# Selective scan: units of 32 channels by 16 states instead of 96 channels by 4, two groups of states in one scan instruction

## The chip, the cores and the metric

One core of a Trainium2 chip runs the whole program in one launch. The metric is device time in microseconds, the median of three runs. All numbers are 32-bit floats.

## The reference, cut to what matters

The model takes a batch of 8 images of 64x64 positions and 96 channels through four residual layers. Layers 0 and 2 are vision state-space layers with a selective scan, layer 1 is a chunked variant of it, layer 3 works on frequencies. The change lies in layers 0 and 2, so the scan runs 2 x 8 = 16 times in a launch. What it computes, for each image and each of K = 4 directions (rows, columns, and both backwards), over D = 192 channels, N = 16 states and L = 4096 positions:

```python
delta = softplus(delta + delta_bias)           # delta, B, C: projections of u
def step(h, inp):
    ut, dt, bt, ct = inp
    dA = jnp.exp(dt[..., None] * A4)           # decay, channel x state
    dBu = (dt * ut)[..., None] * bt[:, :, None, :]
    h = h * dA + dBu
    y = jnp.einsum('bkdn,bkn->bkd', h, ct)
    return (h, y)
...
return y + u * D[None, :, None]                # the four directions are added up
```

`u` is the output of a depthwise 3x3 convolution with SiLU.

## The kernel before, in words

An image's layer goes through `project` (norm and first projection), `selective_scan` and, at the start of the next layer, `back` (gate, norm, output projection, residual). `selective_scan` begins with the convolution: VectorE does rows 0 to 40 (`conv`, line 248), TensorE rows 40 to 64 in three blocks of 8 rows (`conv_pe`, line 264) with diagonal weights that GpSimd builds (`diagonals`, line 258). Each block's sums lie in the two banks named `pu`, of which there is one buffer, until ScalarE has applied SiLU.

Then come 32 steps: 4 directions by 8 chunks of 512 positions (`steps`). A step is 8 units: two halves of 96 channels, and in each four groups `g` of 4 states. On the 128 partitions lie 32 channels by 4 states; the third index `q` is a 32-channel third of the half. A unit does:

- `decays` (line 508): ScalarE writes three tiles `da` = exp(delta x A) into three PSUM banks, from `dx`, delta repeated over the states.
- `with_b` (line 520) and `with_b2` (line 528): `db` = delta x u x B. VectorE makes thirds 0 and 1, reading delta x u from the banks `pu`, where TensorE has spread it over the partitions (`spread`, line 498); GpSimd makes third 2 from `du2`.
- three scans of 512 columns on VectorE (line 633), which begin from the last column of the chunk before (`state`).
- `hc` = h x C for all three thirds on GpSimd (line 645).
- `total_y` (line 534): three matmuls with `red` add up the 4 states of a group into bank `py`. Four units fill it; then `add_y` (line 549) adds it to `y` on VectorE.

The inputs of a step are made by the generator `prepare` (line 429), one part at a time, beside the units of the step before (`PARTS`, line 25: parts at units -2, -1, 0, 1, 3 and 4, counted from that step's start). TensorE projects B and C (`pb`) and delta (`pv`) in two banks of their own, tag `misc`. ScalarE copies B and C to `bcs` and makes `delta` by softplus. Since B, C and delta must be repeated over partitions, they go to DRAM (`bcd`, `dd`, `dud`) and come back with a repeating source: `bc` (2 MB, two buffers), `dx` (0.79 MB a half, three buffers), `du2` (0.52 MB, two buffers). All of these are issued on the SyncE (SP) queue in program order.

The order on every engine is the order written in the code (`manual_schedule`); waits are put in where one tile's use needs them. Pools decide when a buffer comes free.

Of the kernel before, what the change touches and what calls it, by code (L numbers as in the profile page):

```python
# [24 lines left out]
PARTS = (-2, -1, 0, 1, 3, 4)  # L25
# [39 lines left out]
def tile_vision_stack(  # L65
# [51 lines left out]

    eps = wp.tile([128, 1], F32, name="eps")
# [29 lines left out]
    b2 = wp.tile([128, DM], F32, name="b2")  # L148
    with (
# [3 lines left out]

        wdts = []
        for i, (dtw, dtx) in enumerate(((dt0, dx0), (dt2, dx2))):
            left = sp.tile([RK, K * 192], F32, name="left")
            nc.sync.dma_start(left, dtx)
            right = sp.tile([RK, K * 192], F32, name="right")
            nc.sync.dma_start(right, dtw)
            wdt = wp.tile([DM, K, 2, 192], F32, name=f"wdt{i}")  # L160
            for k in range(K):
                pw = pp.tile([DM, 2, 192], F32, name="pw", bufs=2)
                for hf in range(2):
                    nc.tensor.matmul(
                        pw[:, hf, :],
                        left[:, k * 192 + hf * 96 : k * 192 + hf * 96 + 96],
                        right[:, k * 192 : k * 192 + 192],
                        start=True,
                        stop=True,
                    )  # L170
                nc.vector.tensor_copy(wdt[:, k, :, :], pw)
            wdts.append(wdt)
# [221 lines left out]
    def selective_scan(w, wdt, a, d, u, y):  # L394
# [11 lines left out]
        xproj = w[:, C_XP : C_XP + K * 2 * XR].rearrange("p (k j r) -> p k j r", k=K, j=2)  # L406
# [6 lines left out]
        units = 2 * NSG  # L413
        total = len(steps) * units
        with (
# [6 lines left out]
            tc.tile_pool(name="p_du", bufs=1, space=PSUM) as pup,  # L422
            tc.tile_pool(name="p_da", bufs=3, space=PSUM) as pap,
# [5 lines left out]
            def prepare(i):  # L429
# [4 lines left out]
                m = made[i] = {}  # L434
                pb = pmp.tile([128, 2, LC], F32, name="pb", tag="misc")
                for hf in range(2):
                    nc.tensor.matmul(
                        pb[:32, 0, :],
                        xproj[:, k, hf, RK:XR],
                        uv[hf],  # L440
                        start=(hf == 0),
                        stop=(hf == 1),
                    )
                yield
                bcs = tp.tile([32, LC], F32, name="bcs")
                nc.scalar.copy(bcs, pb[:32, 0, :])  # L446
                bcd = dp.tile([32, LC], F32, name="bcd")
                nc.sync.dma_start(bcd, bcs)
                pv = pmp.tile([128, 2, LC], F32, name="pv", tag="misc")
                for hf in range(2):  # L450
                    for hi in range(2):
                        nc.tensor.matmul(  # L452
                            pv[:DM, hf, :],
                            wdt[:, k, hi, hf * 96 : hf * 96 + 96],
                            uv[hi],
                            start=(hi == 0),
                            stop=(hi == 1),
                        )
                    yield

                m["bc"] = bc = cp.tile([128, 2 * NSG, LC], F32, name="bc")
                src = bcd.rearrange("(j n) l -> n j l", n=4)
                for n in range(4):
                    nc.sync.dma_start(
                        bc[32 * n : 32 * n + 32],
                        src[n : n + 1].to_broadcast([32, 2 * NSG, LC]),
                    )
                delta = tp.tile([DM, 2, LC], F32, name="delta")
                for hf in range(2):
                    bias = w[:, C_DTB + 2 * k + hf : C_DTB + 2 * k + hf + 1]  # L470
                    nc.scalar.activation(delta[:, hf, :], pv[:DM, hf, :], AF.Softplus, bias=bias)
                dd = dp.tile([192, LC], F32, name="dd")
                m["dx"] = []

                def repeat(hf):
                    nc.sync.dma_start(dd[hf * 96 : hf * 96 + 96], delta[:, hf, :])
                    dx = cp.tile([128, 3, LC], F32, name="dx", bufs=3)
# [4 lines left out]

                repeat(0)
                yield
                m["du"] = du = tp.tile([DM, 2, LC], F32, name="du")
                for hf in range(2):
                    nc.gpsimd.tensor_mul(  # L487
                        cut(du[:, hf, :], wh), cut(delta[:, hf, :], wh), uv[hf]
                    )
                dud = dp.tile([32, 2, LC], F32, name="dud")  # L490
                nc.sync.dma_start(dud, du[64:96])
                m["du2"] = du2 = cp.tile([128, 2, LC], F32, name="du2")
# [4 lines left out]

            def spread(t):

                m, hf = made[t // units], t % units // NSG  # L500
                m["pu"] = pu = pup.tile([128, 2, LC], F32, name="pu")
                for q in range(2):
                    rows = slice(32 * q, 32 * q + 32)
                    nc.tensor.matmul(  # L504
                        pu[:, q, :], sel[rows, :], m["du"][rows, hf, :], start=True, stop=True
                    )

            def decays(t):
                m, (k, _) = made[t // units], steps[t // units]
                hf, g = t % units // NSG, t % NSG  # L510
                m["da", t] = []
                for q in range(3):
                    da = pap.tile([128, LC], F32, name="da")
                    at = 3 * hf + q
                    nc.scalar.activation(  # L515
                        da, m["dx"][hf][:, q, :], AF.Exp, scale=av4[:, k, at, g : g + 1]
                    )
                    m["da", t].append(da)

            def with_b(t):  # L520
                m, g = made[t // units], t % NSG
                db = gp.tile([128, 2, LC], F32, name="db", bufs=2)
                nc.vector.tensor_mul(  # L523
                    db, m["pu"], m["bc"][:, g : g + 1, :].to_broadcast([128, 2, LC])
                )
                m["db", t] = db

            def with_b2(t):
                m, hf, g = made[t // units], t % units // NSG, t % NSG
                db = gp.tile([128, LC], F32, name="db2")  # L530
                nc.gpsimd.tensor_mul(db, m["du2"][:, hf, :], m["bc"][:, g, :])  # L531
                m["db2", t] = db

            def total_y(t):

                m, hf, g = made[t // units], t % units // NSG, t % NSG
                hc = m.pop(("hc", t))
                if g == 0:
                    sums.append((pyp.tile([DM, LC], F32, name="py"), hf, steps[t // units]))
                for q in range(3):  # L540
                    nc.tensor.matmul(  # L541
                        sums[-1][0][32 * q : 32 * q + 32, :],
                        red,
                        hc[:, q, :],
                        start=(g == 0),
                        stop=(g == NSG - 1),
                    )

            def add_y():
                py, hf, (k, c) = sums.pop(0)  # L550
                yv = view(y[:, hf, :], k % 2 == 1, c * LC, LC)
                if k == 0:
                    nc.vector.scalar_tensor_tensor(
                        yv, u[:, hf, c * LC : c * LC + LC], d[:, hf : hf + 1], py, ALU.mult, ALU.add
                    )
                else:
                    nc.vector.tensor_add(yv, yv, cut(py, k % 2 == 1))

            parts = {}
            for i in range(len(steps)):
                for n, at in enumerate(PARTS):
                    parts.setdefault(units * (i - 1) + at, []).append(i)
            going = {}

            def prepare_parts(t):
                for i in parts.get(t, ()):
# [5 lines left out]
            dg = cp.tile([128, 2 * NSG, LC], F32, name="bc").rearrange("p a b -> p (a b)")  # L574
            dg = dg[:DM, : 18 * DM].rearrange("p (n m) -> p n m", n=18)
            diagonals(dg, w)
            first = list(range(-units + PARTS[0], 0))

            def conv_block(n):
                acc = pup.tile([128, 2, LC], F32, name="pu")[:DM]  # L580
                for hf in range(2):
                    conv_pe(dg, y, n, hf, acc[:, hf, :])
                return n, acc

            def silu_block(n, acc):
                for hf in range(2):
                    silu(w, u, (8 * n, 8 * n + 8), hf, acc[:, hf, :])

            for hf in range(2):
                conv(w, y, u, (0, 8), hf)  # L590
            for _ in range(5):
                prepare_parts(first.pop(0))
            done = conv_block(5)
            for n, rows in ((6, (8, 24)), (7, (24, 40))):
                for hf in range(2):
                    conv(w, y, u, rows, hf)
                    if n == 6 and hf == 0:
                        prepare_parts(first.pop(0))
                        prepare_parts(first.pop(0))
                silu_block(*done)  # L600
# [715 lines left out]
```

## Time and profile before

| | |
|---|---|
| median of three runs | 32904.44 us (32891.0 to 32913.84) |
| the profiled execution | 32953.56 us, its span 32951.8 us |
| busy share of the span | VectorE 81%, TensorE 72%, GpSimd 70%, ScalarE 46% |
| granted TensorE clock, mean | 0.696 of full |
| products h x C on GpSimd (L645) | 14165.5 us, 4096 of 3458 ns |
| scans (L633) | 12980.4 us (10752 of 1261 ns) and 1762.9 us (1536 of 1203 ns) |
| DMA | 2672.97 MB, mean 81 GB/s |

A line of a group names the line of the code, the engine, the operation, output and inputs with their shapes and a count; then the busy time in us, the mean of one in ns, and how long the engine stood idle just before these instructions, with what ended most of it. PE is TensorE, PEld its weight loads, DVE VectorE, ACT ScalarE, POOL GpSimd, SP the queue that issues transfers. A timeline line begins with the start in us and the time in us. By the timeline of GpSimd a step takes 39.4 us where u is read in rows and 39.9 us where it is read in columns; 512 steps are over 60% of the span.

### The profile page before, as it was taken

What the parts mean: (1) busy time and instruction counts of PE and PEld (TensorE: products, weight loads), DVE (VectorE), ACT (ScalarE), POOL (GpSimd) and SP (SyncE); (2) the same over time, 40 slices, a digit from 0 to 9 for tenths busy, and PEclk for the clock granted to TensorE, in tenths of its full rate; (3) what the DMA queues carried; (4) which work ended last, traced back from release to release, by engine and by line L of the source; (5) the groups of instructions that cost most, each with busy time, mean ns of one, the idle gap of its engine ahead of it and who ended that gap; (6) DMA issues with size and microseconds to landing.
All of it is one profiled execution on the core that took longest, in us unless ns stands there. A gap on an engine that the chain in (4) does not pass through costs nothing. (4 is left out here: it accounts for less than half of the span.)

```text
span 32951.8 us, 294593 instructions
## 1 busy us (share of the span) xinstructions
PE 23737.3 (72%) x90246; PEld 8381.8 (25%) x90246; DVE 26605.5 (81%) x27030; ACT 15241.2 (46%) x24909; POOL 23212.3 (70%) x12908
## 2 busy tenths in 40 slices
PE   6686766967668676686766967668676686766867
PEld 1141311413114131141311413114131141311413
DVE  9859698596986969859698596985969859698696
ACT  5435454354543545435454354543545435454354
POOL 8739587395874949739487395873948739497494
PEclk6676766767667676676766767767676676766767
DMA  5315253152431525315253152531525315253152
GB/s 114 85 26 122 59 113 86 25 121 60 112 87 29 121 62 113 82 29 121 57 114 83 25 121 60 113 85 27 121 59 114 84 28 121 59 115 83 30 122 57
DMA packets 1461625, 2672.97 MB, mean 81 GB/s; under 512 B 271544, under 2 KB 271768, under 8 KB 1460048
## 3 DMA queue, kind: packets, MB, share of 16 engines
q1 hardware_dynamic: 1443408, 2647.83, 36.0%
q8 instruction: 724, 11.86, 0.2%
q10 hardware_dynamic: 16640, 6.29, 0.1%
q14 instruction: 853, 6.99, 0.1%
HBM read 2271.62 MB, written 381.68 MB: 81 GB/s over the span
## 5 line engine op out<-in xcount | busy, mean ns | idle before, releaser
L645 POOL TENSOR_TENSOR hc<-h,bc 128x1536 f32<-128x1536 f32 x4096 | 14165.5, 3458 | 678.1 <-DVE h L633 676.5
L633 DVE TENSOR_TENSOR_SCAN h<-da,state,db 128x512 f32<-128x512 f32 x10752 | 12980.4, 1261 | 102.5 <-POOL hc L645 100.7
L541 PE MATMUL py<-hc,cst 128*32 128x512 f32 x24576 | 6836.1, 905 | 7754.8 <-POOL hc L645 7100.7
L515 ACT ACTIVATE da<-dx,a2s 128x512 f32<-128x512 f32 x6144 | 4208.3, 690 | 4489.7 <-DVE h L633 4486.1
L515 ACT ACTIVATE da<-dx,a0s 128x512 f32<-128x512 f32 x6144 | 4208.3, 690 | 4489.2 <-DVE h L633 4485.1
L523 DVE TENSOR_TENSOR db<-pu,bc 128x1024 f32<-128x1024 f32 x4096 | 4931.0, 1204 | 597.6 <-ACT da L515 415.1
L531 POOL TENSOR_TENSOR db<-du,bc 128x512 f32<-128x512 f32 x4096 | 5330.2, 1301 | 103.5 <-DMA du<-dud 103.5
L541 PEld LDWEIGHTS py<-hc,cst 128*32 128x32 f32 x24576 | 805.3, 129 | 13702.4 <-POOL hc L645 13459.6
L452 PE MATMUL pv<-u,wdt 96*96 96x512 f32 x4096 | 2932.4, 845 | 22.0 <-ACT bcs L446 22.0
L226 POOL TENSOR_SCALAR xn<-xs,sb 96x512 f32<-96x512 f32 x192 | 215.2, 1127 | 3215.7 <-DVE sb L206 3078.3
L818 POOL TENSOR_TENSOR rr<-lr,cst 128x768 f32<-128x768 f32 x256 | 433.3, 1693 | 2354.1 <-ACT lr L816 1231.2
L887 ACT ACTIVATE sg<-sg 128x768 f32<-128x768 f32 x1024 | 819.3, 800 | 2467.3 <-PE sg L871 2467.3
L504 PE MATMUL pu<-du,cst 32*128 32x512 f32 x4096 | 1848.0, 994 | 4.0 <-DVE db L523 4.0
L633 DVE TENSOR_TENSOR_SCAN h<-da,db 128x512 f32<-128x512 f32 x1536 | 1762.9, 1203 | 62.5 <-POOL hc L645 60.7
L487 POOL TENSOR_TENSOR du<-delta,u 96x512 f32<-96x512 f32 x1024 | 1445.0, 1443 | 0.0
L919 DVE TENSOR_TENSOR wt<-wt,cbm 128x768 f32<-128x768 f32 x1024 | 1092.8, 1087 | 352.0 <-ACT wt L888 348.5
L957 PE MATMUL py<-wt,xdt 128*32 128x128 f32 x12288 | 1024.4, 334 | 230.0 <-DVE y L995 154.2
L1078 DVE SCALAR_TENSOR_TENSOR f<-p,w3bs,f 128x512 f32<-128x512 f32 x768 | 576.4, 750 | 726.1 <-ACT f L1071 699.1
L965 PE MATMUL py<-ce,state 96*96 96x128 f32 x3968 | 1124.6, 373 | 0.0
L452 PEld LDWEIGHTS pv<-u,wdt 96*96 96x96 f32 x4096 | 615.9, 170 | 1903.2 <-issue 1410.0
L292 POOL TENSOR_SCALAR xn<-xs,sb 96x512 f32<-96x512 f32 x192 | 156.6, 818 | 1318.4 <-issue 953.3
L871 PE MATMUL sg<-rr,lr 32*128 32x384 f32 x4096 | 1073.3, 644 | 0.0
(201 smaller groups left out, 31992.8 us busy)
## 6 DMA issues: line engine op xcount, KB each, us to landing
bc<-bcd SPq DMA_DIRECT2D x2048, 512.0 KB, 10.1
dx<-dd SPq DMA_DIRECT2D x4096, 192.0 KB, 3.6
du<-dud SPq DMA_DIRECT2D x2048, 128.0 KB, 2.7
dd<-delta SPq DMA_DIRECT2D x1024, 192.0 KB, 4.3
dud<-du SPq DMA_DIRECT2D x512, 128.0 KB, 1.9
xd<-xs SPq DMA_DIRECT2D x256, 192.0 KB, 2.1
bcd<-bcs SPq DMA_DIRECT2D x768, 64.0 KB, 1.6
xs<-xd SPq DMA_DIRECT2D x128, 384.0 KB, 5.8
```

Source lines behind the costliest of these rows:

```text
L452: nc.tensor.matmul(pv[:DM, hf, :], wdt[:, k, hi, hf * 96 : hf * 96 + 96], uv[hi], start=(hi == 0), stop=(hi == 1),)
L487: nc.gpsimd.tensor_mul(cut(du[:, hf, :], wh), cut(delta[:, hf, :], wh), uv[hf])
L504: nc.tensor.matmul(pu[:, q, :], sel[rows, :], m["du"][rows, hf, :], start=True, stop=True)
L515: nc.scalar.activation(da, m["dx"][hf][:, q, :], AF.Exp, scale=av4[:, k, at, g : g + 1])
L523: nc.vector.tensor_mul(db, m["pu"], m["bc"][:, g : g + 1, :].to_broadcast([128, 2, LC]))
L531: nc.gpsimd.tensor_mul(db, m["du2"][:, hf, :], m["bc"][:, g, :])
L541: nc.tensor.matmul(sums[-1][0][32 * q : 32 * q + 32, :], red, hc[:, q, :], start=(g == 0), stop=(g == NSG - 1),)
L633: nc.vector.tensor_tensor_scan(h[:, q, way], das[q][:, way], db2[:, way] if q == 2 else db[:, q, way], init, ALU.mult, ALU.add,)
L645: nc.gpsimd.tensor_mul(hc, h, m["bc"][:, NSG + g : NSG + g + 1, :].to_broadcast([128, 3, LC]))
L871: nc.tensor.matmul(live[e]["sg"][:, p, :3, :], m["lr"][rows, 0, :], m["rr"][rows, 3 * p : 3 * p + 3, :], start=True, stop=True,)
L919: nc.vector.tensor_mul(it["wt"], it["wt"], m["cbm"][:, j : j + 1, :].to_broadcast([128, RK, Q]),)
L965: nc.tensor.matmul(py[:, i, hf, :], it["before"][:, 96 * hf : 96 * hf + 96], m["ce"][:, j, :], start=False, stop=True,)
```

## The change

A unit is now 32 channels by all 16 states, so that a step has 6 units (`units = NCG`) instead of 8. The four groups of 4 states lie side by side in the free dimension, 513 apart (`SEG`): 512 positions, and one place in between.

- `db` and `h` are tiles of 4 x 513 + 1 columns. The place ahead of each group holds the state from the chunk before, written into `db` by ScalarE (`enter`), and `da` holds 0 there; so one scan instruction runs over two groups, 1026 columns, from an initial 0.0, and restarts in the middle. A unit is two scans instead of three.
- `da` is two PSUM tiles of 1027 columns, one for each pair of groups.
- `with_b` is one instruction of 4 x 512 columns a unit: on VectorE for four units of a step, on GpSimd for the two with `n % 3 == 2`.
- The product with C (`leave`) is one instruction of 4 x 512 on GpSimd and is done in place, `h` by `h`; ScalarE's copy of the last column goes before it. `h` has five buffers.
- `total_y` runs once per half, after its third unit: 12 matmuls with `red`, behind one that starts the sum with `y` itself (identity) or, in direction 0, with u x D (`skip`). ScalarE copies the bank to `y`; the two sums on VectorE (`add_y`) are gone.
- The projections use the one bank of the sums (tag `py`), delta's second half by itself, and its first half together with B and C as 128 columns of weights (`wdts`, which lie in DRAM and are loaded at the start of each layer). They are copied to `raw1` and `raw0`; softplus works in place.
- `bc` is split: `c` has two buffers, `b` one. `dx` has two instead of three, `du2` one instead of two. The parts of `prepare` are eight: raw1's matmuls in unit 4 of the step before the previous one, its copy in unit 5; then, in the previous step, raw0's matmuls in unit 1, its copy with `bcd` and `c` in unit 2, softplus with `dd` and the first `dx` in unit 2, `b` in unit 3, du with `dud` and `du2` in unit 4, the second `dx` in unit 5.
- In the prologue the blocks of the convolution on TensorE have two buffers of their own (`p_conv`), and block 6 is issued before the SiLU of block 5.

The core of the diff:

```diff
-        units = 2 * NSG
+        units = NCG
...
+                yield
+                raw0 = tp.tile([128, LC], F32, name="raw0")
+                nc.scalar.copy(raw0, pv)
                 bcd = dp.tile([32, LC], F32, name="bcd")
-                nc.sync.dma_start(bcd, bcs)
+                nc.sync.dma_start(bcd, raw0[DM:])
+                def copies(at, pool, name):
+                    t = pool.tile([128, NSG, LC], F32, name=name)
+                    src = bcd[at : at + NST].rearrange("(g n) l -> n g l", n=4)
+                    for n in range(4):
+                        nc.sync.dma_start(
+                            t[32 * n : 32 * n + 32],
+                            src[n : n + 1].to_broadcast([32, NSG, LC]),
+                        )
+                    return t
-                m["bc"] = bc = cp.tile([128, 2 * NSG, LC], F32, name="bc")
...
+                m["c"] = copies(NST, cp, "c")
+                yield
+                delta = [raw0[:DM], raw1[:DM]]
...
+                    nc.scalar.activation(delta[hf], delta[hf], AF.Softplus, bias=bias)
...
+                nc.sync.dma_start(dd[:DM], delta[0])
                 repeat(0)
+                nc.sync.dma_start(dd[DM:], delta[1])
                 yield
+                m["b"] = copies(0, tp, "b")
+                yield
...
+            def enter(t):
+                i, n = t // units, t % units
+                k, c = steps[i]
+                first = c == (0 if k < 2 else NCH - 1)
+                db = gp.tile([128, NSG * SEG + 1], F32, name="db")
+                src = zero if first else states[i - 1][:, NSG * n : NSG * n + NSG]
+                nc.scalar.copy(places(db, NSG, int(k >= 2)), src)
+                made[i]["db", n] = db
...
+            def with_b(t):
+                m, n = made[t // units], t % units
+                pool = n % 3 == 2
+                (nc.gpsimd if pool else nc.vector).tensor_mul(
+                    groups(m["db", n]),
+                    (m["du2"][:, n // 3, :] if pool else m["pu"])
+                    .unsqueeze(1).to_broadcast([128, NSG, LC]),
+                    m["b"],
+                )
...
+            def scan(t, p):
...
+                at = slice(2 * p * SEG + rev, 2 * (p + 1) * SEG + rev)
+                if p == 0:
+                    made[i]["h", n] = gp.tile([128, NSG * SEG + 1], F32, name="h", bufs=5)
+                nc.vector.tensor_tensor_scan(
+                    made[i]["h", n][:, at][:, way],
+                    das[p][:, rev : 2 * SEG + rev][:, way],
+                    made[i]["db", n][:, at][:, way],
+                    0.0, ALU.mult, ALU.add,
+                )
+            def leave(t, more):
...
+                nc.scalar.copy(
+                    states[i][:, NSG * n : NSG * n + NSG], h[:, :, 0 if k >= 2 else LC - 1]
+                )
+                if more:
+                    prepare_part(i + 1)
+                nc.gpsimd.tensor_mul(h, h, made[i]["c"])
...
+                for t in range(total + 2):
+                    n, i = t % units, t // units
+                    ahead = t + 1 < total
+                    if n == 1 and t + 2 < total:
+                        spread(t + 2)
+                    elif n in (0, 3, 5) and ahead:
+                        spread(t + 1)
+                    if n == 0 and i > 0:
+                        sums = total_y(i - 1, 1)
+                    elif n == 3:
+                        sums = total_y(i, 0)
+                    elif n == 1:
+                        prepare_part(i + 1)
+                    elif n == 4:
+                        prepare_part(i + 2)
+                    if t < total:
+                        scan(t, 0)
+                        if n % 3 == 0 and t + 2 < total:
+                            with_b(t + 2)
+                    if ahead:
+                        decays(t + 1, 0)
+                    if n % 3 == 1 and t > 1:
+                        nc.scalar.copy(*sums)
+                    if t < total:
+                        scan(t, 1)
+                        leave(t, n == 4)
+                    if t + 3 < total:
+                        enter(t + 3)
+                    if ahead:
+                        decays(t + 1, 1)
+                        if (n + 1) % 3 != 2:
+                            with_b(t + 1)
+                    if n == 2:
+                        prepare_part(i + 1)
+                        prepare_part(i + 1)
+                    elif n == 3:
+                        prepare_part(i + 1)
+                    elif n == 5:
+                        prepare_part(i + 1)
+                        prepare_part(i + 2)
```

## The prediction, made before the changed kernel was run

> **What bounds the kernel now.** I read the page first, then the busy time by windows inside one scan, the timelines of GpSimd and of the DMA queue over one step, and the DMA rate in slices of 2 us. The page's costliest groups:
>
> ```profile
> L645 POOL TENSOR_TENSOR hc<-h,bc 128x1536 f32<-128x1536 f32 x4096 | 14165.5, 3458 | 678.1 <-DVE h L633 676.5
> L633 DVE TENSOR_TENSOR_SCAN h<-da,state,db 128x512 f32<-128x512 f32 x10752 | 12980.4, 1261 | 102.5 <-POOL hc L645 100.7
> L523 DVE TENSOR_TENSOR db<-pu,bc 128x1024 f32<-128x1024 f32 x4096 | 4931.0, 1204 | 597.6 <-ACT da L515 415.1
> L531 POOL TENSOR_TENSOR db<-du,bc 128x512 f32<-128x512 f32 x4096 | 5330.2, 1301 | 103.5 <-DMA du<-dud 103.5
> L633 DVE TENSOR_TENSOR_SCAN h<-da,db 128x512 f32<-128x512 f32 x1536 | 1762.9, 1203 | 62.5 <-POOL hc L645 60.7
> ```
>
> 4096 units are 512 steps of 8. Busy time by windows in the first scan (PE, PEld, DVE, ACT, POOL, clock, DMA share, GB/s):
>
> ```profile
> 160.00:1390.00 1230.00, 775.93 (x2096) 133.15 (x2096) 1208.21 (x1053) 669.37 (x1142) 1230.00 (x558) 0.64 0.53 119
> ```
>
> GpSimd never rests, VectorE rests 1.8%, DMA is half idle. A step is 18 GpSimd instructions, so 558 are 31 steps: **39.67 us a step**. The GpSimd timeline gives pitches (start to start):
>
> ```profile
> 713.62 3.06 POOL L487 TENSOR_TENSOR du<-delta,u 96x512 f32<-96x512 f32 x2
> 716.59 3.50 POOL L645 TENSOR_TENSOR hc<-h,bc 128x1536 f32<-128x1536 f32 x1
> 720.00 1.32 POOL L531 TENSOR_TENSOR db<-du,bc 128x512 f32<-128x512 f32 x1
> 721.22 3.49 POOL L645 TENSOR_TENSOR hc<-h,bc 128x1536 f32<-128x1536 f32 x1
> ```
>
> 1536 columns take 3.4 us, 512 take 1.23: 2.11 ns a column and 0.15 fixed. The two du take 2.97 here, 2.45 where u is read in rows.
>
> Now the DMA queue in one step, and the DMA share and GB/s (last two columns) of slices inside it:
>
> ```profile
> 730.78 0.31 SPq L448 DMA_DIRECT2D bcd<-bcs  x1
> 733.97 2.88 SPq L464 DMA_DIRECT2D bc<-bcd  x4
> 741.06 0.31 SPq L476 DMA_DIRECT2D dd<-delta  x1
> 749.54 1.72 SPq L480 DMA_DIRECT2D dx<-dd  x4
> ```
> ```profile
> 734.00:736.00 2.00, 2.00 (x9) 0.63 (x10) 2.00 (x3) 0.50 (x3) 2.00 (x2) 1.00 0.29 88
> 736.00:738.00 2.00, 0.95 (x3) 0.09 (x1) 2.00 (x2) 1.27 (x2) 2.00 (x1) 1.00 0.87 126
> 738.00:740.00 2.00, 0.50 (x6) 0.18 (x6) 2.00 (x3) 1.75 (x3) 2.00 (x3) 1.00 1.07 167
> 740.00:742.00 2.00, 2.00 (x10) 0.30 (x4) 2.00 (x3) 1.97 (x4) 2.00 (x1) 0.72 0.90 190
> 742.00:744.00 2.00, 1.07 (x5) 0.19 (x6) 2.00 (x3) 1.99 (x3) 2.00 (x2) 0.50 1.05 209
> 744.00:746.00 2.00, 1.17 (x6) 0.00 (x0) 2.00 (x3) 0.96 (x3) 2.00 (x2) 0.50 1.07 202
> 746.00:748.00 2.00, 0.14 (x3) 0.14 (x6) 2.00 (x3) 1.16 (x2) 2.00 (x2) 0.50 0.59 131
> 748.00:750.00 2.00, 1.78 (x6) 0.06 (x3) 2.00 (x3) 1.03 (x3) 2.00 (x2) 0.50 0.11 34
> ```
>
> This is the view that decides. The eight slices move 2.29 MB, which is bc (2.10) and the small dd (0.19), at about 200 GB/s once full. The dd store is issued at 741.06, yet dx, which reads dd back, goes out only at 749.54: a small store queues behind the big load, and the issue queue stands until it has landed. Here nobody waits: bc has two buffers, dx three.
>
> **The compute engines, part by part.** *GpSimd.* The columns stay: 6 products with c and 2 with b of 2048 instead of 8 of 1536 and 8 of 512. At 2.11 ns and 0.15 each is 4.47 us: 35.8 + 2.7 (du) = 38.5 us, 1.2 less, eight fixed costs. No row has groups at a step of 513; the row nearest in kind that reads its operand in steps is du at 1.48 against 1.22, so 38.5 to 46; I take 38.5, since only one hop in 512 columns is new.
>
> *VectorE.* 12 scans of 1026 columns that start from 0.0: twice the pitch of 512 is 2.24, less the fixed part; I take 2.2 (2.1 to 2.4). Four products of 2048: 2.2 each (row L523: 1.12 for 1024). Sum 35.2 against 8 x (1.12+3.54) + two sums into y (0.64 to 1.16 each) = 39.6. So VectorE alone would run 4.4 us faster.
>
> *ScalarE* gets the two copies into y (0.58 by the copies of a 96x512 bank) and initial values (0.18 each); 24 exponentials at 0.62 leave it some 60% busy. *TensorE.* The sums of a half come as 12 matmuls after its third product, four triples of 1.71 us at half clock, 7 us, plus an identity matmul ahead, which doesn't need h. Its cover: between product 5 and product 1 GpSimd has two instructions (8.9 us) and the way over TensorE (7.0), the copy (0.6) and the state copy (0.2) takes some 8.3; hidden, by 0.6. If the cover is gone it is a stall of that size.
>
> **The DMA chain, where I put the time.** The projections of the next step now share the bank of the sums, so bcs becomes raw0, copied only in unit 2, behind both exponentials of unit 3, which wait for unit 2's second scan. Call its end X. And b has one buffer, loaded behind c, dx and two dd stores in the in-order issue queue:
> - raw0 ready: state 0.18, initial value 0.18, two exponentials 1.3, copy 0.57, handoffs: X+2.4.
> - bcd stored, c issued 1.9 later (60.82 to 62.73 in the first prologue): X+4.3.
> - bc to dx took 15.6 (733.97 to 749.54); c is 1.05 MB less, 5.2 us at 200 GB/s (by the slices 1.25 MB are through after 8.5, and landed after 9.5): 10.0, so dx leaves at X+14.3.
> - dx (0.79 MB) took 4.5 until its slices end at 754: X+18.8. The second dd, 0.19 MB: X+19.8. b, 1.05 MB at 200 GB/s: X+25.0, landed X+25.7.
> - VectorE's product of unit 0 waits for b, and behind it stand all scans. From it to the end of unit 2: two products and six scans, 8 x 2.2 = 17.6. That end is the next X.
>
> A step is thus **43.3 us**. Whatever is late for 38.5 on GpSimd hides in this. Bounds: at 167 GB/s (slice 738) c and b take 1.1 longer each, 45.5; at 253, the best slice seen with dx (764 to 766), 1.1 shorter each, 41.1. The end on the other side is b hidden: it must be there by X+20.9 for GpSimd's 38.5, by X+22.6 to match today. The next loads, dud and du, follow b by some 6 us, but GpSimd needs them only for unit 2, 11 us after b: hidden.
>
> *A rule against this reading.* The Trainium skill, "DMA: Bandwidth & Descriptors", section "Bandwidth", puts the 16 engines' ceiling near 436 GB/s. By it the chain's 3.28 MB would need 7.5 us instead of 16.4, b would be there before X+17, and the change would win as in the first rival. The slices above, full at 200, speak against it.
>
> **The prologue** gains. VectorE ends its share of the convolution at 107.0 and stands still until 133.44 (26.41 us, 16 times 415.1 in the row of L523), because the third convolution block on TensorE waits for the bank of the second until 109.41 and takes 18.3. With two banks it follows the second (85.22 + 15.5, plus 1.7 for a projection) and ends near 118; SiLU, table and two exponentials later the first scan starts at about 121.3, not 135.7. Between nothing and 20 us gained; I take 14.
>
> **Sum.** First X: 121.3 + one product and six scans = 136.7. Then 31 x 43.3, and behind the last X five GpSimd instructions, 22.8: 1501.8, where today the last product ends at 1406.7. That is 95.1 more in each of 16 layers, 1520 us. The profiled execution takes 32953.6 (span 32951.8), 49 above the median of 32904.4: 34474 there, **34425** as a median. By the chain's bounds and the prologue's, 33300 to 35600.
>
> **Rivals.** *The chain is hidden and GpSimd bounds* (transfers run faster when halved, or overlap). Start of products at 125.9 + 4 of stalls + 32 x 38.5 - 4.5 = 1357, 50 less a layer: about 32100, faster. For it: 128 to 192 KB loads land in 2.7 to 3.6 us. Against: the slices. It decides below X+22.6. *dd doesn't queue behind c*: then volume alone counts, 5.6 + 16.4 + 0.7: b at X+22.7, a step of 40.3, 32940. For it: dd lands in 4.3 at the median. Against: 8.5 behind bc. *c and b crawl* at 126 GB/s, the slice of 736: 3.1 longer each, 49.5, 37500; against it, that slice is the ramp.
>
> **How the numbers follow.** The chain 0.70; hidden 0.12; dd beside c 0.13, a third of it on each side of no change; crawling 0.05. About 0.2% is what a measurement can tell. Faster 0.16, same 0.04, slower 0.80. Half of the hidden case and the crawl stay outside 32700 to 35700.
>
> **What would show it.** Right: VectorE idle some 8 us a step before its product with b of unit 0, released by the DMA of b; GpSimd no longer at 100% and waiting for scans or du; 2048 columns at 4.5 us, scans at 2.2; SP waiting for dd about 7 us a step. Wrong: GpSimd at 100%, or VectorE waiting for GpSimd or TensorE instead, or products with c well above 4.5 us.

## The result: no gain and no loss worth naming, and the profile after

The changed kernel takes 32878.98 us (median of 12), the kernel before 32916.47 in the same runs: a ratio of 0.9984, interval 0.9972 to 0.9996. That is 0.16% faster, less than the 0.2% that the prediction took as the least a measurement can tell. The forecast was 34425, slower by 4.6%, so the likeliest case was wrong by 1550 us. The time lies below the 33300 to 35600 that came from the bounds of the chain and the prologue, and only inside the wider 32700 to 35700 of the chances. The profiled execution below took 32765.36 (span 32763.6).

The costliest groups, which answer to those shown of before (line engine op, shapes, count | busy, mean ns | idle before, what ended it):

```profile
L572 DVE TENSOR_TENSOR_SCAN h<-da,db 128x1026 f32<-128x1026 f32 x6144 | 13651.3, 2278 | 210.0
L593 POOL TENSOR_TENSOR h<-h,c 128x2048 f32<-128x2048 f32 x3072 | 12784.8, 4169 | 620.3 <-ACT state L588 490.6
...
L542 DVE TENSOR_TENSOR db<-pu,b 128x2048 f32<-128x2048 f32 x2048 | 4654.1, 2272 | 2062.5 <-DMA b<-bcd 2057.1
...
L542 POOL TENSOR_TENSOR db<-du,b 128x2048 f32<-128x2048 f32 x1024 | 4648.7, 4540 | 1705.4 <-PE pu L536 644.8
```

Busy time of the engines in the window of the first scan that was shown of before (PE, PEld, DVE, ACT, POOL, clock, DMA share, GB/s):

```profile
160.00:1390.00 1230.00, 817.02 (x2094) 185.03 (x2094) 1093.85 (x494) 726.48 (x1343) 1123.39 (x307) 0.69 0.48 118
```

GpSimd worked all of the 1230.00 us before; now it works 1123.39, and VectorE went from 1208.21 to 1093.85. Both have less to do and both stand still for over 100 us. What VectorE stands still for is in its group: 2057.1 us in front of the product with b, ended by the DMA of b. That is the wait which the prediction named. The timeline of VectorE in one step (start, duration, instruction, idle before it) shows it come once a step:

```profile
737.43 2.27 DVE L542 TENSOR_TENSOR db<-pu,b 128x2048 f32<-128x2048 f32 x1
739.80 4.48 DVE L572 TENSOR_TENSOR_SCAN h<-da,db 128x1026 f32<-128x1026 f32 x2
744.20 2.27 DVE L542 TENSOR_TENSOR db<-pu,b 128x2048 f32<-128x2048 f32 x1
746.57 8.85 DVE L572 TENSOR_TENSOR_SCAN h<-da,db 128x1026 f32<-128x1026 f32 x4
760.02 2.29 DVE L542 TENSOR_TENSOR db<-pu,b 128x2048 f32<-128x2048 f32 x1 [4.60 <-DMA b<-bcd]
```

The queue of SyncE in the same step:

```profile
739.69 0.31 SPq L465 DMA_DIRECT2D bcd<-raw  x1
741.35 1.73 SPq L472 DMA_DIRECT2D c<-bcd  x4
743.18 0.38 SPq L493 DMA_DIRECT2D dd<-raw  x1
748.58 1.72 SPq L490 DMA_DIRECT2D dx<-dd  x4
750.39 0.37 SPq L495 DMA_DIRECT2D dd<-raw  x1
750.87 1.91 SPq L472 DMA_DIRECT2D b<-bcd  x4
```

The small store dd is issued right behind c, and dx, which reads it back, leaves 5.4 us later. So the chain raw0, bcd, c, dd, dx, dd, b is there, in the forecast's order. But from c to dx it takes 7.23 us here, where 10.0 had been forecast. The slices of 2 us of that stretch (the last two columns are the DMA share and GB/s):

```profile
741.00:743.00 2.00, 2.00 (x3) 0.39 (x2) 2.00 (x2) 1.98 (x3) 2.00 (x2) 0.50 0.19 60
743.00:745.00 2.00, 2.00 (x7) 0.39 (x9) 2.00 (x2) 1.96 (x4) 2.00 (x1) 0.50 0.97 256
745.00:747.00 2.00, 2.00 (x15) 0.52 (x12) 1.90 (x2) 1.54 (x5) 2.00 (x2) 0.87 1.06 222
```

From 1.65 to 3.65 us after the first issue of c 256 GB/s are moved, and then 222. Before, bc had only 126 from 2.03 to 4.03 us after its first issue, and then 167: this load comes up to its full rate sooner. A step, from one issue of bcd to the next, is 40.03 us on average over 26 steps of the first scan, against 39.75 before.

### The profile page after: what moved, and what is told of

It is laid out like the page before. It is cut to its first block, busy times and chain, and to the rows that moved or that the text cites. A ratio compares the mean times of both kernels' runs of the same rounds, so it can differ in the third digit from the quotient of the medians.

```text
span 32763.6 us, 279135 instructions
## 1 busy us (share of the span) xinstructions
PE 24399.9 (74%) x90246; PEld 9157.0 (28%) x90246; DVE 24776.0 (76%) x17921; ACT 16308.8 (50%) x28493; POOL 21606.8 (66%) x8844
## 5 line engine op out<-in xcount | busy, mean ns | idle before, releaser
L572 DVE TENSOR_TENSOR_SCAN h<-da,db 128x1026 f32<-128x1026 f32 x6144 | 13651.3, 2278 | 210.0
L593 POOL TENSOR_TENSOR h<-h,c 128x2048 f32<-128x2048 f32 x3072 | 12784.8, 4169 | 620.3 <-ACT state L588 490.6
L536 PE MATMUL pu<-du,cst 32*128 32x512 f32 x4096 | 3574.0, 966 | 5275.1 <-DVE db L542 5222.9
L542 DVE TENSOR_TENSOR db<-pu,b 128x2048 f32<-128x2048 f32 x2048 | 4654.1, 2272 | 2062.5 <-DMA b<-bcd 2057.1
L542 POOL TENSOR_TENSOR db<-du,b 128x2048 f32<-128x2048 f32 x1024 | 4648.7, 4540 | 1705.4 <-PE pu L536 644.8
L610 PE MATMUL py<-h,cst 128*32 128x512 f32 x24576 | 5307.4, 801 | 61.0 <-POOL h L593 61.0
L448 PE MATMUL pv<-u,wdts 96*96 96x512 f32 x2048 | 1461.5, 841 | 1101.7 <-ACT state L588 567.6
L458 PE MATMUL pv<-u,wdts 96*128 96x512 f32 x2048 | 1504.1, 864 | 585.2 <-ACT state L588 325.5
L600 PE MATMUL py<-y,cst 96*96 96x512 f32 x1536 | 1551.3, 1108 | 39.6 <-ACT state L588 39.6
L501 POOL TENSOR_TENSOR du<-raw,u 96x512 f32<-96x512 f32 x1024 | 1435.4, 1423 | 0.0
```

The source lines that it names most:

```text
L448: nc.tensor.matmul(pv[:DM], wdts[:, k, hi, 128:], uv[hi], start=(hi == 0), stop=(hi == 1))
L458: nc.tensor.matmul(pv, wdts[:, k, hi, :128], uv[hi], start=(hi == 0), stop=(hi == 1))
L501: nc.gpsimd.tensor_mul(cut(du[:, hf, :], wh), cut(delta[hf], wh), uv[hf])
L536: nc.tensor.matmul(pu, sel[rows, :], m["du"][rows, n // 3, :], start=True, stop=True)
L542: (nc.gpsimd if pool else nc.vector).tensor_mul(groups(m["db", n]), (m["du2"][:, n // 3, :] if pool else m["pu"]) .unsqueeze(1) .to_broadc ...
L572: nc.vector.tensor_tensor_scan(made[i]["h", n][:, at][:, way], das[p][:, rev : 2 * SEG + rev][:, way], made[i]["db", n][:, at][:, way], 0. ...
```

## The experiments

Theory A: the DMA chain closes the step; its length from c to dx goes one for one into the step. Theory B, the rival: the half-step sums on TensorE, the in-place product or the five buffers of h set the step, and VectorE's wait for b only fills time that would be lost anyhow.

**c behind b.** The loads of c leave the chain:

```diff
-                m["c"] = copies(NST, cp, "c")
                 yield
...
                 m["b"] = copies(0, tp, "b")
+                m["c"] = copies(NST, cp, "c")
```

> The changed kernel with one thing moved: the four loads of c are issued behind those of b instead of ahead of the first dd store. Theory A (the DMA chain from raw0 to b closes the loop of a step, 40.1 us in the trace of the changed kernel): dd no longer queues behind c, b lands some 17 to 18 us after the second scan of unit 2, about when VectorE comes to it; a step of 36.5 (VectorE and GpSimd together) to 38.5 (GpSimd then waits for du2, which now queues behind c); about 31600 us, ratio to before 0.96. Theory B (the sums of a half, five buffers of h and the in-place product bound the step, the wait for b only fills the gap): nothing moves, 32880, ratio 0.998.

Measured: 31731.74 us, ratio 0.9639 (0.9618 to 0.9661), a step of 37.86. With nothing large ahead of it dd let dx go after 2.08 us on average, not 5.5. So A holds: B had forecast that nothing moves. The step isn't quite the sum of GpSimd's own instructions yet, which is 36.5 us. In the timeline of GpSimd over this step one wait is left:

```profile
735.42 4.53 POOL L542 TENSOR_TENSOR db<-du,b 128x2048 f32<-128x2048 f32 x1 [1.58 <-DMA du<-dud]
```

This wait is not new: the store dud, which GpSimd's du2 comes from, stands behind c here and takes 5.3 us to land. In the changed kernel it stood behind b and took 6.2, and in the kernel before it took 1.9 (medians of the three pages).

**raw0 early.** The chain stays as it is, but starts earlier, ahead of unit 2's second scan:

```diff
+                    if n == 2:
+                        prepare_part(i + 1)
                     if t < total:
                         scan(t, 1)
...
                     if n == 2:
                         prepare_part(i + 1)
-                        prepare_part(i + 1)
```

> The changed kernel with raw0 copied, and bcd and c issued, ahead of the state copy of unit 2 instead of behind both exponentials of unit 3. Theory A: the chain starts 2.3 us earlier, the step goes from 40.1 to 37.8; 31750 us, ratio 0.965. Theory B: nothing gained, and state and product of unit 2 come 0.6 us later: 32880 to 33150.

Measured: 31710.58 us, ratio 0.9627 (0.9613 to 0.9641), a step of 37.71, with c to dx unchanged at 7.36 us. One line of the timeline of VectorE, which begins at X of this kernel, and one of the queue, show the head start:

```profile
742.38 2.27 DVE L542 TENSOR_TENSOR db<-pu,b 128x2048 f32<-128x2048 f32 x1
743.92 1.73 SPq L472 DMA_DIRECT2D c<-bcd  x4
```

c goes out 1.5 us after X, in the changed kernel 3.9: 2.4 us earlier, and the step is 2.3 us shorter. By itself this run couldn't rule out B, because the copy of raw0 also frees the bank that raw0 shares with the sums, and so does it earlier. But c behind b leaves the sums, the product and the buffers of h as they are and gives nearly the same gain, so they can't have been the bound.

**The old prologue.** The other part of the change that moves time, undone:

```diff
-            with tc.tile_pool(name="p_conv", bufs=2, space=PSUM) as pvp:
+            with tc.tile_pool(name="p_conv", bufs=1, space=PSUM) as pvp:
...
-                blocks = [conv_block(5)]
-                conv(w, y, u, (8, 24), 0)
...
+                done = conv_block(5)
+                for n, rows in ((6, (8, 24)), (7, (24, 40))):
...
+                    silu_block(*done)
+                    done = conv_block(n)
```

> The changed kernel with the prologue of before: one buffer for the banks of the convolution on TensorE, and its blocks and SiLUs in the old order. If the prologue gave what the first layer's trace says (first scan at 122.0 instead of 135.7, 13.7 us in each of 16 layers): 220 us more than the changed kernel, 33100, ratio to before 1.005. If the gain is swallowed later: 32880.

Measured: 33014.43 us, ratio 1.0025 (1.0016 to 1.0035), so the prologue is worth some 135 us of the changed kernel's 32879, 8.5 us a layer. Without it the change would have been a small loss. Its first scan starts at 128.60, in the changed kernel at 122.03, before at 135.71: half of that gain is the bank and the order, and half is there without them. The 220 us expected had counted the whole of it.

**bc of the kernel before in eight loads.** This asks where the 10.0 went wrong. The kernel before, with the same 2.10 MB of bc in 8 transfers of 256 KB instead of 4 of 512:

```diff
-                for n in range(4):
-                    nc.sync.dma_start(
-                        bc[32 * n : 32 * n + 32],
-                        src[n : n + 1].to_broadcast([32, 2 * NSG, LC]),
-                    )
+                for at in (NSG, 0):
+                    for n in range(4):
+                        nc.sync.dma_start(
+                            bc[32 * n : 32 * n + 32, at : at + NSG, :],
+                            src[n : n + 1, at : at + NSG, :].to_broadcast([32, NSG, LC]),
+                        )
```

> The kernel before with the 2 MB load bc issued as eight transfers of 256 KB (C's rows, then B's) instead of four of 512 KB; nothing else. If transfers of 256 KB over four rows move faster by themselves, the first dx goes out 11.5 to 13 us after the first of bc instead of 15.6. If the rate comes from what else runs in the changed kernel, it stays at 15 to 16. Time in both cases as before, 32900, since nobody waits for bc there.

Measured: 32919.46 us (one run), a step of 39.75 as before, because nobody waits for this load there. What counts is the queue, in this kernel's step, and then two slices of the load:

```profile
731.60 3.62 SPq L465 DMA_DIRECT2D bc<-bcd  x8
738.70 0.31 SPq L477 DMA_DIRECT2D dd<-delta  x1
744.07 1.72 SPq L481 DMA_DIRECT2D dx<-dd  x4
```
```profile
733.00:735.00 2.00, 1.57 (x4) 0.33 (x2) 2.00 (x3) 1.00 (x2) 2.00 (x1) 1.00 0.89 237
735.00:737.00 2.00, 0.00 (x0) 0.00 (x0) 2.00 (x3) 1.50 (x4) 2.00 (x2) 1.00 1.05 214
```

From bc to dx it is 12.47 us here, 15.57 in the step that the prediction quotes (12.8 against 15.2 on average over the first scan). The same bytes go through 3.1 us sooner, and the slices show where: from 1.4 us after the first issue 237 GB/s are moved and then 214, where the four large transfers had 126 and 167. Once at full rate both kernels move about the same, 209 and 202 before, 212 and 206 here. And 12.47 less 1.05 MB at the forecast's 200 GB/s, 5.2, is 7.2: what the changed kernel needs. The rate was right; the 15.57 from which it was subtracted contained 3.1 us (2.4 on average) that belong to transfers of 512 KB and not to the bytes. Size and number of the transfers change together here; the run doesn't say which of them it is.

**c twice.** The chain made longer by 1.05 MB:

```diff
                 m["c"] = copies(NST, cp, "c")
+                src = bcd[NST : 2 * NST].rearrange("(g n) l -> n g l", n=4)
+                for n in range(4):
+                    nc.sync.dma_start(
+                        m["c"][32 * n : 32 * n + 32],
+                        src[n : n + 1].to_broadcast([32, NSG, LC]),
+                    )
```

> The changed kernel with c loaded twice into the same tile, both times ahead of the dd store (1.05 MB more in the queue each step, nothing else changed). Theory A (the chain raw0, bcd, c, dd, dx, dd, b closes the step): c to dx grows from 7.2 us to 12.4 (1.05 MB more at the 200 GB/s that the first comparison of 8 and 4 quarter-megabyte loads gave), or some 1 us more if the second load waits for the first; the step from 40.1 to 45.3 to 46.5, 32 x 16 x 5.2 to 6.4 = 2660 to 3280 us more: 35500 to 36200, ratio 1.08 to 1.10. Theory B (sums of a half, in-place product or buffers of h bound the step): less than 0.5% more, under 33050.

Measured: 35270.79 us (one run), a step of 45.03. The queue, in this kernel's step:

```profile
773.32 1.73 SPq L472 DMA_DIRECT2D c<-bcd  x4
776.98 3.90 SPq L481 DMA_DIRECT2D c<-bcd  x4
780.92 0.42 SPq L499 DMA_DIRECT2D dd<-raw  x1
785.50 1.75 SPq L496 DMA_DIRECT2D dx<-dd  x4
```

From c to dx it is 12.18 here, 4.95 more than in the step of the changed kernel shown above, and the step is 5.00 longer on average. The second load was held up by the first: its issue takes 3.90 us instead of 1.73, so the 4.95 aren't a clean price of the bytes. The total came out somewhat under the 35500 to 36200 expected.

**c in eighths**, and **c by groups of states.** Two other shapes of the same load, to see whether a smaller transfer goes on gaining and whether its size is all that counts. The loop of c in the first, and in the second:

```diff
+                    width = 16 if at else 32
+                    for p in range(0, 128, width):
+                        n = p // 32
                         nc.sync.dma_start(
-                            t[32 * n : 32 * n + 32],
-                            src[n : n + 1].to_broadcast([32, NSG, LC]),
+                            t[p : p + width],
+                            src[n : n + 1].to_broadcast([width, NSG, LC]),
                         )
```

```diff
+                        if at:
+                            rows = bcd[at + 4 * n : at + 4 * n + 4].unsqueeze(1)
+                            nc.sync.dma_start(t[:, n, :], rows.to_broadcast([4, 32, LC]))
+                            continue
```

> The changed kernel with c loaded in 8 transfers of 128 KB (16 partitions each), not 4 of 256 KB. If smaller transfers go on gaining as from 512 KB to 256 KB (3.1 us in 15.6 for twice the bytes, so 1.5 here), c to dx falls to some 5.7 and the step to 38.6, 32100. If bytes set the pace at this size already (1.05 MB at 200 GB/s and 2 us of start), c to dx stays at 7.0 to 7.5 and the time at 32700 to 33000. If the issue of eight (3.4 us, not 1.7) holds dd back, c to dx is 7.5 to 8.5, 33000 to 33500.

> The changed kernel with c loaded by groups of states: 4 transfers of 256 KB as before, but each writes one row of 2 KB to all 128 partitions and not four rows to 32. If the size of a transfer is what made c to dx shorter than I forecast (7.2 us, not 10.0), this changes nothing: 7.0 to 7.5, a step of 40.1, 32700 to 33000. If the number of partitions that a transfer covers matters, it moves by more than 0.7 us, and the step with it (0.7 us a step is 360 us in all): under 32500 or above 33200.

Measured: 34071.84 us for the eighths, 35682.61 for the groups (one run each). c to dx takes 9.88 us in eighths and 13.08 by groups on average. So smaller transfers don't go on gaining: the eighths are slower than all three cases of their expectation. And size is not all that counts: the groups have transfers of the same size as the change. Slices of 2 us show two different reasons (DMA share and GB/s at the end). In eighths:

```profile
744.00:746.00 2.00, 2.00 (x15) 0.35 (x9) 2.00 (x1) 0.00 (x0) 2.00 (x1) 0.93 1.09 137
```

and by groups:

```profile
747.00:749.00 2.00, 0.00 (x0) 0.00 (x0) 2.00 (x2) 1.64 (x3) 2.00 (x1) 1.00 0.26 101
```

In eighths all 16 DMA engines are busy and move 137 GB/s where the quarters moved 222 at about the same share (1.06): the packets take longer. The issue takes longer too, so that dd goes out 3.8 us after the first of c instead of 1.8, and it then waits 6.1 us instead of 5.5. As the engines are full before and after dd goes out, the packets are the likelier reason for the 9.88; no run separates the two. By groups only 0.26 of the engines work. The Trainium skill, page "DMA: Bandwidth & Descriptors", section "Why a DMA increments its semaphore by 16 and not by 1", says that a transfer is spread over the largest number of engines up to 16 that divides the slowest dimension of both its sides. Here the source's slowest dimension is 4, which would make 4 of 16 engines, 0.25, as an estimate from that page. The 0.26 agrees.

The four lengths of the chain, with the rest of the kernel unchanged (averages over the first scan):

| c loaded as | c to dx, us | step, us | step less c to dx | time, us |
|---|---|---|---|---|
| 4 x 256 KB, 32 partitions (the change) | 7.34 | 40.03 | 32.7 | 32878.98 |
| 8 x 128 KB, 16 partitions | 9.88 | 42.76 | 32.9 | 34071.84 |
| 4 x 256 KB, twice | 12.11 | 45.03 | 32.9 | 35270.79 |
| 4 x 256 KB, by groups | 13.08 | 45.82 | 32.7 | 35682.61 |

The last column but one is constant within 0.2 us: over a range of 5.7 us what the chain gains or loses between c and dx is the step's, one for one.

**Both mends.** raw0 early, and the queue in the order bcd, dd, dx, dd, b, dud, du2, c. So c stands further back than in the first experiment, behind du2 too; that place was not run by itself:

```diff
-                m["c"] = copies(NST, cp, "c")
                 yield
...
                     nc.sync.dma_start(du2[32 * n : 32 * n + 32], dud)
+                m["c"] = copies(NST, cp, "c")
...
+                    if n == 2:
+                        prepare_part(i + 1)
                     if t < total:
                         scan(t, 1)
...
-                        prepare_part(i + 1)
```

> Both mends together: raw0 copied before unit 2's second scan, and the queue in the order bcd, dd, dx, dd, b, dud, du, c, so that no load of a megabyte stands before what the step waits for. Theory A: b lands before VectorE wants it and du before GpSimd wants it; GpSimd's own sum, 36.5 us, is the step (36.5 to 36.9, from 37.7 with either mend alone): 31100 to 31300, ratio 0.945 to 0.951. Theory B: no better than one mend alone, 31700, ratio 0.963, with GpSimd or VectorE waiting for each other or for TensorE.

Measured: 31140.1 us, ratio 0.9463 (0.9447 to 0.9479), a step of 36.83. Its queue, and then its engines in a window inside the first scan:

```profile
730.48 0.31 SPq L492 DMA_DIRECT2D dd<-raw  x1
732.52 1.73 SPq L489 DMA_DIRECT2D dx<-dd  x4
```

```profile
180.00:1280.00 1100.00, 802.22 (x2031) 197.25 (x2030) 1061.62 (x480) 712.48 (x1316) 1092.63 (x301) 0.71 0.53 131
```

dd lands and lets dx go after 2.0 us. GpSimd works 1092.63 of 1100.00 us, 99.3%; with c behind b alone it was 1060.45 in the same window, in the changed kernel 1006.41. GpSimd is the bound again, now with the shorter sum of the new units, and this kernel beats both others: the one before by 5.4%, the changed one by 5.3% (31140.1 against 32878.98).

## Why the prediction was wrong

**The step that failed: "15.6 less 5.2 us at 200 GB/s: 10.0, so dx leaves at X+14.3".** It measured 7.23 in the step shown, 7.34 on average. Two causes hide in one time: the bytes, whose price was right (5.2 us a megabyte also separates the eight loads of bc from the four of c), and the shape in four transfers of 512 KB, 3.1 us of the 15.6 (2.4 on average), which went away with the halving. The sum carried that part over as if it belonged to any load. Its second working, "by the slices 1.25 MB are through after 8.5", did the same, because it read the slow start of the large transfers. And its bounds changed only the rate, 167 to 253 GB/s, and never the start, so that the measured step of 40.0 lies below its lower end of 41.1. With this term at 9.88 us, as it is with c in eighths, the kernel takes 34071.84, 1.0% under the forecast and 3.5% slower than before: the forecast's own case exists, only the change isn't it.

**The rest of the chain held.** Counted from X = 737.43, the end of unit 2's second scan: c goes out at X+3.9 (forecast 4.3), from the issue of dx to the landing of b 11.4 us (forecast 11.4), from VectorE's product of unit 0 to the next X 17.9 (17.6). The one term makes the step 40.5 there instead of 43.3.

**Which case it was.** The measured time is nearly that of the rival "dd doesn't queue behind c" (32940), but that mechanism didn't happen: dd waits 5.5 us behind c and 2.1 without it. Nor was the chain hidden: VectorE waits 4 us for b in each step (some 8 had been forecast), and SyncE 5 to 5.4 for dd (7). It is the forecast's first case with a smaller number. That the result is so close to no change, and to that rival, is chance: the shorter chain happens to use up just what the engines and the prologue gain.

**The engines.** Scans take 2.19 us from start to start (forecast 2.2), products with b on VectorE 2.37 to the start of the scan behind them (2.2), so 35.8 in all against 35.2. GpSimd: 4.50 for the product with b (4.47), but 4.13 for the product with c, so its sum is 36.5 and not 38.5. That error was without effect while the chain decides; with both mends it is the reason why the step gets to 36.8. The cover of the sums on TensorE (the time in which GpSimd has other work) was enough: with the chain out of the way GpSimd rests for 0.7%.

**The prologue.** The first scan starts at 122.03 (forecast 121.3). Of the 13.7 us gained, undoing the bank and the order takes back 6.6: the other half comes from elsewhere in the change, and which part of it was not tried.

**The rule on bandwidth.** The Trainium skill's ceiling of 436 GB/s (page "DMA: Bandwidth & Descriptors", section "Bandwidth") was not reached: the highest slice of 2 us in the step shown moves 271 (752 to 754). The slices were the better guide, but a slice taken during one shape of transfer doesn't carry over to another shape.

## What to carry to other kernels

A load's time read from a trace is that of its shape: bytes, size of a transfer and partitions in one; before part of it is taken off, look for the same bytes in another shape, or measure that. Where a step writes a small tile to DRAM and reads it back, put the store ahead of the large loads in the queue and the large loads behind whatever the step waits for: here that order and an earlier start turn a change of no effect into a gain of 5.4%. When engines with less to do stand still, ask which chain closes the loop from one step to the next; a change of its length that returns one for one in the step is the proof.

## What the runs showed of the hardware

- The same 2.10 MB, rows of 2 KB repeated to 32 partitions a transfer, take 15.2 us in four transfers and 12.8 in eight, to the landing of the small store behind them. With 1.05 MB it is 7.3 us in four transfers, 9.9 in eight of half the size (16 partitions each). Of the shapes run, 256 KB on 32 partitions is the best; why packets are slower in the smaller transfers, and why 512 KB starts more slowly, is open.
- A transfer whose source has only four rows in its slowest dimension keeps a quarter of the DMA engines busy (0.26, 101 GB/s).
- A store of 0.19 MB lands and releases its reader in 2.0 us with no large load ahead of it on the queue, and in 5.5 right behind a load of 1.05 MB.
- GpSimd's product of 2048 columns takes 4169 ns with c and 4540 ns where one factor is repeated over the groups (du2): 9% more, for the repeated operand, for the sources, or because the first is done in place; the runs don't separate these.
